# Graph attention on one core: PSUM copies moved from VectorE to ScalarE in the 8-head layers, and reciprocals split from their small products

## The chip, the cores and the metric

The kernel runs on one core of a Trainium2 chip. The time is device microseconds of one execution. Five engines work side by side: TensorE (PE in the profile; its weight loads are PEld), VectorE (DVE), ScalarE (ACT), GpSimd (POOL) and SyncE (SP, which only issues transfers here). Matrix products are written to PSUM, which has eight banks per partition; DVE and ACT copy them from there to SBUF, the working memory.

## The reference, cut to what matters

Four graph layers follow one another on 3327 nodes with 512 features. Each is wrapped as `x = layernorm(x + layer(x, adj))`. Layers 0 and 2 are graph attention with 8 heads of 64 features, layer 3 with 4 heads of 128; layer 1 averages over the first 64 neighbours. The change touches the attention layers:

```python
def _L2_gnn_ref(h, adj, W, a):                      # layer 0 is the same without elu
    Wh = (h @ W).reshape(n, H, D)                   # H = 8, D = 64
    s1 = jnp.einsum('nhd,hd->nh', Wh, a1)
    s2 = jnp.einsum('nhd,hd->nh', Wh, a2)
    e = jax.nn.leaky_relu(s1[:, None, :] + s2[None, :, :], negative_slope=0.2)
    att_logits = jnp.where(adj[:, :, None] > 0, e, NEG_BIG)
    attention = jax.nn.softmax(att_logits, axis=1)
    h_prime = jnp.einsum('ijh,jhd->ihd', attention, Wh)
    return jax.nn.elu(h_prime.reshape(n, H * D))
```

## The kernel before

**The attention without a softmax pass.** With f1 and f2 the two scores of a node, the weight exp(leaky_relu(f1_i + f2_j)) is exp(f1_i) * d_j * max(r_i, q_j), with r = exp(-0.8 f1), q = exp(0.8 f2) and d = exp(0.2 f2). The factor of i cancels in the quotient. So a tile `t` = max(r_i, q_j) * mask (DVE, one instruction, line 396) times v_j = d_j Wh_j gives the sums: products `po` on PE (line 405). The denominators need only to know which side of the maximum won: ACT turns `t` into a step `y` in 8 bits (line 399), and PE multiplies it by pieces of d and d*q (`pd`, line 365).

**Units.** Nodes are padded to 3328 = 26 tiles of 128. The receiving nodes i are cut into two halves of 1664 = 13 tiles, the features into 4 slots of 128: two heads per slot in the 8-head layers (`HS == 2`), one in the 4-head layer. One call of `unit` handles one half and one slot: 8 calls per attention layer, 24 in all. A unit has 26 steps j, one per tile of sending nodes. Per step and head there is one `t` of 128 x 1664 on DVE, one `y` on ACT, and four `po` products, one per PSUM bank (the 1664 columns are cut as 448, 448, 384, 384). At odd j from 3 on, the `pd` products of steps j-3 and j-2 follow; those of the last two steps come after the loop.

**Buffers.** `t` has 3 buffers per head (6 in the 8-head layers), `y` 7 in layer 0, 8 in layer 2 and 4 in layer 3. The row vectors r, spread over all partitions (`rb`, 832 KB each by DMA, issued by POOL), have HS + 1 = 3 buffers in the 8-head layers: the first head of the next unit is loaded ahead, the second when the present unit's first head has been used for the last time. The `po` banks have one buffer each, so the next unit's `po` products wait for the copies of this unit's.

**Between units.** After the loop the four `po` banks are copied to `ob`: bank 0 by DVE (line 423), banks 1 to 3 by ACT (line 421). After the last slot of a half the denominators are copied from the two `pd` banks to `db`: the lower 64 partitions by ACT (line 452), the upper 64 by DVE (line 453). What is left is returned as a list of jobs that run inside the *next* unit, one per step j, behind that step's `po` and `pd` products: two empty ones, then (after a half) `reciprocals`, then transposes of `ob` (`pt`, copied to `hb` and stored to `hd`) at every second step. `reciprocals` is 26 records of small products `pe` from `db` on PE (line 460), then on DVE, per head of a slot, a multiplication (line 468) and an addition (line 469), and one reciprocal (line 471) into `rec`. After the last unit of a layer the jobs run one after the other.

**Order.** The instruction order on PE is the order of the program text (`manual_schedule` for that engine). On DVE, ACT, POOL and SP a planner orders the instructions when the program is built, by dependencies and its own time estimates; `tc.keep_in_program_order(ins)` ties one instruction behind the instruction that was traced before it on the same engine. At the end of layers 0 and 2 the finishing work of the first two node tiles (`finish`: division by `rec`, layer norm, and elu in layer 2, lines 180 to 194 and 152 to 161) is traced in the last unit, and the planner places parts of it in earlier units.

Of the kernel before, what the change touches and what calls it, by code (L numbers as in the profile page):

```python
# [13 lines left out]
ALU = mybir.AluOpType  # L14
# [18 lines left out]
def kernel(  # L33
# [10 lines left out]
    nc = tc.nc  # L44
# [11 lines left out]
    WA, WB = NA * P, IW - NA * P  # L56
# [48 lines left out]
    for e in range(2):  # L105
        nc.vector.tensor_tensor(c1w[:, :, e, :], c1[:, :, 8 * e:8 * e + 4], c1[:, :, 8 * e + 4:8 * e + 8],
                                op=ALU.add)
# [115 lines left out]
    class Layer:  # L223
# [121 lines left out]
        def unit(self, pools, half, s, background, aside, final=None, ending=None):  # L345
            H, D, HS = self.H, self.D, self.HS
# [4 lines left out]
            for h in heads:  # L351
                r_ = rp.tile([P, IW], F32, name="rb")
# [6 lines left out]
            pd, seen = self.pd, self.seen  # L359
# [57 lines left out]

            ob = sp.tile([P, IW], F32, name="ob", bufs=1)
            for c, (a_, z) in enumerate(CUTS):
                if c:  # L420
                    nc.scalar.copy(ob[:, a_:z], po[c][:, :z - a_])
                else:
                    nc.vector.tensor_copy(ob[:, a_:z], po[c][:, :z - a_])
# [17 lines left out]
            nothing = lambda: None  # L441
            jobs = [nothing, nothing]
# [5 lines left out]
            db = sp.tile([P, WA], F32, name="db", bufs=1)  # L448
            if WB < WA:
                nc.gpsimd.memset(db[64:, WB:], 0.0)  # L450
            for c in range(2):
                nc.scalar.copy(db[:64, c * (WA // 2):(c + 1) * (WA // 2)], pd[c][:64, :WA // 2])
                nc.vector.tensor_copy(db[64:, c * (WB // 2):(c + 1) * (WB // 2)], pd[c][64:, :WB // 2])

            def reciprocals():
                pe = qp.tile([P, HALF, 2, H], F32, name="pe", tag="q")
                for q in range(HALF):
                    e = int(q >= NA)
                    cc = c1[:, :, 8 * e:8 * e + 8] if HS == 2 else c1w[:, :, e, :]
                    nc.tensor.matmul(pe[:, q, :, :], db[:, (q - e * NA) * P:(q - e * NA + 1) * P], cc,  # L460
                                     start=True, stop=True)

                ss = slice(0, NS) if not final else slice(0, 2) if s == 1 else slice(s, s + 1)
                r_ = rec[:, t0:t0 + HALF, :H].rearrange("p t (s k) -> p t k s", k=HS)
                rc = self.rc[:, t0:t0 + HALF, :].rearrange("p t (s k) -> p t k s", k=HS)
                pv = pe.rearrange("p t o (k s) -> p t o k s", k=HS)
                for k in range(HS):
                    nc.vector.tensor_tensor(r_[:, :, k, ss], pv[:, :, 0, k, ss], rc[:, :, k, ss], op=ALU.mult)
                    nc.vector.tensor_tensor(r_[:, :, k, ss], pv[:, :, 1, k, ss], r_[:, :, k, ss], op=ALU.add)
                hs = slice(ss.start * HS, ss.stop * HS)  # L470
                nc.vector.reciprocal(rec[:, t0:t0 + HALF, hs], rec[:, t0:t0 + HALF, hs])

            return jobs[:2] + [reciprocals] + jobs[2:]

# [412 lines left out]
    with tc.tile_pool(name="col0", bufs=1) as cp, tc.tile_pool(name="raw", bufs=2) as rawp:  # L889
        L0.more_columns(cp)  # L890
        L0.piece_columns(cp)
        with tc.tile_pool(name="p_w", bufs=1, reuse_waits="tile") as wp, \
# [37 lines left out]
            held = {}  # L930
# [100 lines left out]
```

## Time and profile before

| | us |
|---|---|
| median of 3 runs | 3499.28 (3495.52 to 3499.89) |
| profiled execution, its own time | 3489.1 |
| its span, first to last instruction | 3486.7 |
| units 0 to 7 (layer 0), first `t` to last `t` | 160.8 to 985.9 |
| units 8 to 15 (layer 2) | 1837.5 to 2628.0 |
| units 16 to 23 (layer 3) | 2761.1 to 3447.7 |
| unit 5, from its first `t` to the next unit's | 97.98 |
| unit 4 (first of layer 0's second half) | 103.12 |
| unit 12 (first of layer 2's second half) | 102.71 |

The mean granted TensorE clock of the profiled execution is 0.983. In the profile's lines, `L396 DVE ... t<-rb,qc,mask` reads: line 396 of the kernel, on VectorE, writing tile `t` from `rb`, `qc` and `mask`; then shapes, the count, and busy time. In a timeline the first number is the start in microseconds from the span's start and the second the duration of the merged run of instructions; brackets give the idle time before and what ended it. Costs below come from this one execution; the changed kernel is compared by medians.

### The profile page before, as it was taken

Reading aid. Unit: us, or ns where it says so; the run is one execution under the profiler, and the core shown is the slowest. Engines: PE = TensorE matmul, PEld = TensorE weight load, DVE = VectorE, ACT = ScalarE, POOL = GpSimd, SP = SyncE. Lnnn points to the kernel's source line nnn. Section 1 sums busy time; section 2 is a strip of 40 time slices with the busy share of each in tenths; the row PEclk is TensorE's granted clock in tenths of the full one; section 3 lists DMA queues with packets and bytes.
Section 4 is the critical chain, followed back from the end, with each engine's and each line's share of the span. In section 5 each row is a group of like instructions: output and inputs, shape, how many; then the busy total and the mean of one; then the engine's idle time right before and its main releaser. Section 6 shows DMA issues by size and latency. Waiting matters only on the chain.

```text
span 3486.7 us, 48120 instructions
## 1 busy us (share of the span) xinstructions
PE 3325.6 (95%) x18873; PEld 1701.2 (49%) x18926; DVE 2694.9 (77%) x2759; ACT 2396.6 (69%) x2336; POOL 181.2 (5%) x289
## 2 busy tenths in 40 slices
PE   6899999999989999999998999999998999999997
PEld 5644444444444455555553444444446754555553
DVE  5599999999967644434439999999998756668886
ACT  1388989899953343433428999899998655558885
POOL 1000000000000111111110000000001000000000
PEclk9999999999999999999999999999999999999998
DMA  9535211101133432222221111111116511112211
GB/s 352 179 104 161 67 44 41 54 27 51 37 105 125 131 90 73 70 61 75 73 66 35 48 47 48 47 46 46 29 39 197 183 33 44 40 46 91 81 38 47
DMA packets 208452, 276.65 MB, mean 79 GB/s; under 512 B 19321, under 2 KB 140355, under 8 KB 208228
## 3 DMA queue, kind: packets, MB, share of 16 engines
q1 hardware_dynamic: 173622, 157.37, 14.1%
q0 software_dynamic: 22736, 89.80, 8.3%
q10 hardware_dynamic: 11870, 26.42, 2.4%
q8 instruction: 149, 2.44, 0.3%
q14 instruction: 75, 0.61, 0.1%
HBM read 204.92 MB, written 68.60 MB: 78 GB/s over the span
## 4 chain that ended last, share of the span: by engine, by line
PE 62%; issue 24%; DVE 6%; DMA 5%; ACT 3%; POOL 1%; POOLq 0%; DVEq 0%; SPq 0%; ACTq 0%
PE po L405 34%; PE acc L728 9%; PE pw L264 5%; PE pd L365 5%; DVE t L396 3%; PE pz L617 2%; PE pi L620 2%; DMA raw<-in_adjT_dram 2%; ACT y L399 1%; DMA cy<-ctd 1%; PE pt L429 1%; PE pk L696 1%; PE pt L253 1%; DVE kt L700 1%; PE pe L460 1%
## 5 line engine op out<-in xcount | busy, mean ns | idle before, releaser
L396 DVE SCALAR_TENSOR_TENSOR t<-rb,qc,mask 128x1664 f32<-128x1664 f32 x1040 | 1960.1, 1947 | 200.8 <-PE po L405 158.6
L399 ACT ACTIVATE y<-t,bi,sc 128x1664 fp8e4<-128x1664 f32 x1040 | 1771.7, 1766 | 341.4 <-PE pd L365 317.4
L405 PE MATMUL po<-t,vj 128*64 128x448 f32 (+3 forms) x8320 | 1939.5, 522 | 26.0 <-DVE t L396 24.6
L405 PEld LDWEIGHTS po<-t,vj 128*64 128x64 f32 (+1 forms) x8320 | 857.8, 148 | 977.7 <-issue 681.1
L728 PE MATMUL acc<-zs,kt 128*128 128x512 bf16 x1314 | 396.6, 381 | 1.9 <-issue 0.4
L264 PE MATMUL pw<-wsb,xT 128*128 128x264 f32 (+1 forms) x1248 | 299.3, 395 | 21.7 <-DVE vt L270 19.5
L688 ACT CAST pk<-cy 128x256 f32<-128x256 bf16 x338 | 124.0, 374 | 272.7 <-DVE kt L700 224.8
L728 PEld LDWEIGHTS <-kt 128*128 128x128 fp8e4 x2028 | 198.8, 98 | 229.6 <-issue 34.5
L264 PEld LDWEIGHTS pw<-wsb,xT 128*128 128x128 f32 x1248 | 238.9, 196 | 65.6 <-issue 18.8
L365 PE MATMUL pd<-y,sden 128*32 128x448 fp8e4 (+1 forms) x4160 | 259.8, 342 | 10.5 <-ACT y L399 10.5
L700 DVE SCALAR_TENSOR_TENSOR kt<-pk,mask 128x256 fp8e4<-128x256 f32 x338 | 140.9, 421 | 159.5 <-PE pk L696 158.9
L728 PE MATMUL acc<-zl,kt 128*128 128x512 bf16 x661 | 252.1, 381 | 1.1 <-DMA zl<-zd 0.5
L365 PEld LDWEIGHTS <-sden 128*32 128x32 bf16 x4160 | 117.8, 96 | 162.4 <-issue 139.8
L270 DVE TENSOR_TENSOR vt<-pw,dc 128x256 f32<-128x256 f32 x156 | 59.1, 418 | 98.1 <-ACT dc L265 93.5
L696 PE MATMUL pk<-mask,upto 128*128 128x256 fp8e4 x338 | 92.5, 274 | 21.1 <-ACT pk L688 20.0
L353 POOL DMA_DIRECT2D rb<-r x40 | 21.5, 539 | 1646.8 <-DVE t L396 1610.1
L268 ACT COPY fc<-pw 128x8 f32<-128x8 f32 (+1 forms) x156 | 22.8, 163 | 112.1 <-PE pw L264 101.8
L617 PE MATMUL pz<-wn,xT 128*128 128x512 f32 x208 | 95.0, 600 | 1.2 <-ACT xT L611 1.2
L620 PE MATMUL pi<-wl,xT 128*128 128x512 f32 x208 | 93.5, 592 | 0.0
L590 POOL DMA_DIRECT2D cy<-ctd x91 | 67.8, 745 | 400.2 <-ACT pk L688 273.5
L708 DVE SCALAR_TENSOR_TENSOR y<-acc,cnt,bnb 128x512 f32<-128x512 f32 x26 | 19.5, 751 | 85.1 <-PE acc L728 85.1
L524 DVE TENSOR_SCALAR mask<-raw 128x832 fp8e4<-128x832 int32 (+2 forms) x86 | 50.2, 592 | 45.0 <-DMA raw<-in_adjT_dram 44.4
(165 smaller groups left out, 1732.2 us busy)
## 6 DMA issues: line engine op xcount, KB each, us to landing
vj<-v SPq DMA_DIRECT2D x312, 128.0 KB
rb<-r POOLq DMA_DIRECT2D x40, 832.0 KB, 4.7
cy<-ctd POOLq DMA_DIRECT2D x78, 256.0 KB, 3.9
v<-vt SPq DMA_DIRECT2D x75, 256.0 KB
h<-hd SPq DMA_DIRECT2D x65, 256.0 KB
raw<-in_adjT_dram ACTq DMA_DIRECT2D x38, 416.0 KB
raw<-in_adjT_dram SPq DMA_DIRECT2D x37, 416.0 KB
hd<-hb SPq DMA_DIRECT2D x60, 256.0 KB
```

The source lines that it names most:

```text
L264: nc.tensor.matmul(pw[e][:, :FW + H], xT[:, c, :], wsb[:, c, e, :], start=c == 0, stop=c == FC - 1)
L365: nc.tensor.matmul(pd[c][32 * kk:32 * kk + 32, :w_], lhsT, rhs, start=(kk, c) not in seen, skip_group_check=final is not None, stop=last a ...
L396: nc.vector.scalar_tensor_tensor(t, rb[k], self.qc[:, j, h:h + 1], mask[:, j, i0:i0 + IW], op0=ALU.max, op1=ALU.mult)
L399: nc.scalar.activation(y, t, AF.Sigmoid, bias=self.bi[:, j, h:h + 1], scale=self.sc[:, j, h:h + 1], saturate=False)
L405: nc.tensor.matmul(po[c][k * D:(k + 1) * D, :z - a_], vj[:, j % 2, k * D:(k + 1) * D], ts[k][:, a_:z], start=j == 0, stop=j == NT - 1)
L590: nc.gpsimd.dma_start(out=cy[:, :n, :], in_=ctd[t:t + n, b * GW:(b + 1) * GW] .rearrange("(o t) i -> o t i", o=1).to_broadcast([P, n, GW]))
L617: nc.tensor.matmul(pz, xT[:, c, :], wn[:, c, :], start=c == 0, stop=c == FC - 1)
L620: nc.tensor.matmul(pi, xT[:, c, :], wl[:, c, :], start=c == 0, stop=c == FC - 1)
L688: nc.scalar.copy(pks[k % 2], carry[b, t // 4 * 4][:, t % 4, :])
L696: nc.tensor.matmul(pk, upto, mask[:, t, i0:i0 + GW], start=False, stop=True, skip_group_check=True)
L700: nc.vector.scalar_tensor_tensor(kt, pk, NEIGHBOURS, mask[:, t, i0:i0 + GW], op0=ALU.is_le, op1=ALU.mult, saturate=False)
L728: nc.tensor.matmul(acc, kts[t][:, s * P:(s + 1) * P], zs[:, t, c, :] if c < 2 else zl[:, t, :], start=t == 0 and c == 0, stop=t == NT - 1 ...
```

## The change

In the 8-head layers all four `po` banks are copied to `ob` by ACT, and both halves of `pd` are copied to `db` by ACT. In all attention layers `reciprocals` is split in two jobs: `sums` (the products `pe`, at the step where `reciprocals` stood) and `reciprocals` (the DVE operations), two steps later, with one empty job between; so the transposes after a half also come two steps later. The multiplications of line 468 are tied behind what was traced before them on DVE.

```diff
             for c, (a_, z) in enumerate(CUTS):
-                if c:
+                if c or HS == 2:
                     nc.scalar.copy(ob[:, a_:z], po[c][:, :z - a_])
                 else:
                     nc.vector.tensor_copy(ob[:, a_:z], po[c][:, :z - a_])
...
             for c in range(2):
                 nc.scalar.copy(db[:64, c * (WA // 2):(c + 1) * (WA // 2)], pd[c][:64, :WA // 2])
-                nc.vector.tensor_copy(db[64:, c * (WB // 2):(c + 1) * (WB // 2)], pd[c][64:, :WB // 2])
-
-            def reciprocals():
+                (nc.scalar.copy if HS == 2 else nc.vector.tensor_copy)(
+                    db[64:, c * (WB // 2):(c + 1) * (WB // 2)], pd[c][64:, :WB // 2])
+            held = []
+
+            def sums():
                 pe = qp.tile([P, HALF, 2, H], F32, name="pe", tag="q")
+                held.append(pe)
                 for q in range(HALF):
...
+            def reciprocals():
+                pe = held[0]
+
                 ss = slice(0, NS) if not final else slice(0, 2) if s == 1 else slice(s, s + 1)
...
                 for k in range(HS):
-                    nc.vector.tensor_tensor(r_[:, :, k, ss], pv[:, :, 0, k, ss], rc[:, :, k, ss], op=ALU.mult)
+                    tc.keep_in_program_order(
+                        nc.vector.tensor_tensor(r_[:, :, k, ss], pv[:, :, 0, k, ss], rc[:, :, k, ss], op=ALU.mult))
                     nc.vector.tensor_tensor(r_[:, :, k, ss], pv[:, :, 1, k, ss], r_[:, :, k, ss], op=ALU.add)
...
-            return jobs[:2] + [reciprocals] + jobs[2:]
+            return jobs[:2] + [sums, nothing, reciprocals] + jobs[2:]
```

## The prediction

> **What bounds the kernel now.** I read the page's busy shares first, then the table by stretches (one 8-head unit per stretch), then the timeline of VectorE (DVE) and ScalarE (ACT) at the start of unit 4 (layer 0, second half, slot 0), then the views of the tiles `rb`, `db` and `ob`, and last the two epilogues of the 8-head layers. A unit is one call of `unit`; I number the 24 calls in order of time: 0 to 7 are layer 0, 8 to 15 layer 2, 16 to 23 layer 3.
>
> ```profile
> PE 3325.6 (95%) x18873; PEld 1701.2 (49%) x18926; DVE 2694.9 (77%) x2759; ACT 2396.6 (69%) x2336; POOL 181.2 (5%) x289
> ```
> ```profile
> core 0: us, PE busy (x) PEld busy (x) DVE busy (x) ACT busy (x) POOL busy (x), PEclk, DMA share, GB/s
> 588.75:691.87 103.12, 101.86 (x728) 44.49 (x727) 99.78 (x61) 91.07 (x62) 1.25 (x3) 0.97 0.15 48
> 691.87:789.85 97.98, 97.79 (x702) 43.28 (x701) 97.98 (x55) 90.43 (x60) 1.06 (x2) 1.00 0.14 44
> 2133.15:2230.95 97.80, 97.01 (x673) 44.42 (x670) 97.48 (x54) 91.19 (x61) 1.06 (x2) 1.00 0.14 44
> 2230.95:2333.66 102.71, 101.34 (x728) 46.81 (x727) 99.79 (x62) 91.64 (x62) 1.26 (x3) 1.00 0.15 47
> ```
> Over the whole span TensorE (PE) looks like the bound. By unit it is not: in unit 5 (691.87 to 789.85) DVE is busy for all 97.98 us. Units 4 and 12, the first after a half, are longer by 5.1 and 4.9 us, and there DVE idles 3.3 and 2.9 us.
>
> ```profile
> 590.62 0.61 DVE L423 COPY ob<-po 128x448 f32<-128x448 f32 x1
> 591.72 5.68 DVE L396 SCALAR_TENSOR_TENSOR t<-rb,qc,mask 128x1664 f32<-128x1664 f32 x3 [0.48 <-DMA rb<-r]
> 597.42 1.03 DVE L453 COPY db<-pd 64x384 f32<-64x384 f32 x2
> 598.49 7.54 DVE L396 SCALAR_TENSOR_TENSOR t<-rb,qc,mask 128x1664 f32<-128x1664 f32 x4
> 608.82 0.21 DVE L468 TENSOR_TENSOR rec<-pe,rc 128x52 f32<-128x52 f32 x1 [2.79 <-PE pe L460]
> ...
> 615.60 3.71 DVE L396 SCALAR_TENSOR_TENSOR t<-rb,qc,mask 128x1664 f32<-128x1664 f32 x2
> ```
> The columns are start, duration, instruction, and in brackets the idle time before it with what ended it. Three things to see: the copy L423 is followed by a wait for the DMA of `rb`; the two copies L453 stand between two `t`; L468 waits 2.79 us for the small products. ACT and PE beside it:
>
> ```profile
> 591.66 1.25 ACT L421 COPY ob<-po 128x448 f32<-128x448 f32 x3
> 593.18 3.44 ACT L399 ACTIVATE y<-t,bi,sc 128x1664 fp8e4<-128x1664 f32 x2 [0.27 <-PE pd L365]
> 596.53 0.94 ACT L452 COPY db<-pd 64x448 f32<-64x448 f32 x2
> 597.36 10.11 ACT L399 ACTIVATE y<-t,bi,sc 128x1664 fp8e4<-128x1664 f32 x6
> 615.88 1.77 ACT L399 ACTIVATE y<-t,bi,sc 128x1664 fp8e4<-128x1664 f32 x1 [8.41 <-PE pd L365]
> ```
> ```profile
> 595.48 6.55 PE L405 MATMUL po<-t,vj 128*64 128x448 f32 x34
> 602.36 3.01 PE L405 MATMUL po<-t,vj 128*64 128x448 f32 x14 [0.33 <-DVE t L396]
> 605.30 3.48 PE L460 MATMUL pe<-c,db 128*128 128x16 f32 x26
> ```
> So here PE waits for DVE (0.33 us) and ACT for PE; DVE sets the pace. One `t` costs DVE (5.68 - 1.95) / 2 = 1.865 us from start to start, and 52 of them 97.0 us of a unit's 98. Against that, the Trainium skill (Perfetto Trace Analysis, Identifying the Most-Contended Engine) says to work on the engine of highest occupancy, while warning that matmul busy time is no good measure for TensorE. By its first half the change, which takes nothing off PE, would give 0 us; the table by unit speaks for the warning.
>
> **Part 1, `ob` copy c = 0 from DVE to ACT, 16 units.** Off DVE go 16 x 0.61 = 9.9 us busy (0.53 each from start to start). Little of it is on the path. The view of `rb` over units 4 to 7 gives:
>
> ```profile
> DMA to landing us min/median/max: 4.2/4.4/5.2
> ```
> The second head's `rb` of the next unit is loaded into the buffer that t(25,0) frees: t(25,0) ends at 586.9, POOL issues at 587.25, the data lands at 591.62. DVE has two `t` to do meanwhile (t(25,1) and the next t(0,0)) and would be ready at 590.6. A hole of 1.0 us stays whatever stands in it: today 0.53 of copy and 0.48 of wait, afterwards 1.0 of wait. Gain 0 at the boundaries that show such a wait. At six (into units 5 to 7 and 13 to 15) the planner also put a 0.6 us step of the finishing work there, so copy plus step take 1.13: the gain is 0.1 each, 0.6 together. If these steps go elsewhere, 6 x 0.5 = 3 us are lost instead.
>
> On ACT a fourth `ob` copy adds 1.25 / 3 = 0.42 us between two `y`, ahead of the last `y` of the unit; the last `pd` products wait for that `y`, and the next unit's first `po` for them. PE thus starts 0.14 (the present 0.27 us of ACT idle absorbs the rest) to 0.42 us later. Cover: `t` has 6 buffers, three steps. In units 2, 3, 5 to 7 and 9 to 15 each `t` begins at least 3.1 us after `y` and `po` had freed its buffer (starts and ends from the timeline), so DVE does not feel it. Cost 0.
>
> **Part 2, `db` upper halves from DVE to ACT, 4 times.** In units 4 and 12 DVE loses L453 between two `t`: 598.49 - 597.36 = 1.13 us each, on the path. ACT gets 2 x 0.47 = 0.94, ahead of the first `y` of the unit; y(3,1) waits 8.4 us for PE anyway, which hides it.
>
> **Part 3, small products and reciprocals apart.** `sums` stays where `reciprocals` was on PE (step 2); DVE's part comes two steps later, behind t(4,1). Unit 4 forward: `rb` lands as before, t(0,1) starts at 591.72; nine `t` later (no L453) DVE is at 591.72 + 9 x 1.865 = 608.5. PE: `po` of steps 0 and 1 from 595.6 to 595.9 on, 6.0 us; t(2,1) ends at 601.1, so step 2 runs at once, to 604.5 to 605.0; `pe` 3.41 more: 607.9 to 608.4. The pinned L468 then waits for nothing, by 0.1 us at the tight end. The five DVE operations cost 1.2 us interleaved, as now, t(5,0) 1.865: t(5,1) starts at 611.6 where it starts at 615.60 now. **Gain 4.0** (2.79 + 1.13 + rounding). Unit 12 the same way: 2233.90 + 16.8 = 2250.7, t(5,1) at 2253.75 instead of 2257.38: **3.6** (2.38 + 1.13).
>
> What is late next: y(3,1) (layer 0 has 7 `y` buffers) waits for the first `pd` products of the unit, which follow step 3 on PE. With `pe` done at 608.3 and 3.0 for step 3, they begin at 611.3, y(3,1) at 612.7 (1.43 after, as now) and ends at 614.5; t(6,1), which takes over the buffer of t(3,1), would start at 611.6 + 3.7 = 615.3. Margin 0.8, today 1.6. If it is gone, DVE idles up to about 1 us there; between 0 and 1.0 I take 0.4, the value if PE starts at its late end. Layer 2 has 8 buffers and margin to spare. The transposes and the `hd` stores move two steps too (PE 0.6, ACT 0.57 and one SP issue every second step): these fall on PE and ACT beside DVE-bound steps, and nothing reads `hd` until later. The 4-head layer gets only the later, pinned reciprocals; there DVE waits on PE (17.1 us of idle before `t` in unit 23 alone), so 0.
>
> **Part 4, the two epilogues.** No `t` follows, so the copies are on the path to `pe`. Layer 0: ACT copies at 995.99 and 996.40, DVE's at 996.54 and 997.05, `pe` from 997.16. With all on ACT and one more `ob` copy ahead, the first pair ends at 995.99 + 0.42 + 0.94 = 997.35 instead of 997.10: +0.2 to +0.4. Layer 2: DVE's first copy is late (2635.54, behind finishing work), ACT could be through at 2635.3: up to -0.8. The view of `db` shows why ACT in series costs so little:
>
> ```profile
>   ACT db L452: 9.0, 4
> ```
> DVE's copy of a bank waits for ACT's of the same bank; they alternate already. The Trainium skill (PSUM — Partial Sum Buffer, Terms, "Quadrant") reports that different quadrants of one bank may be accessed at once. By that the halves could overlap and two more ACT copies would cost their full 0.94 us in each epilogue; no overlap shows here. Against both stands the planner's choice of where the square-root and exponential tables load: layer 0's epilogue has two loads of 1.28 us ahead of the last `y`. Bounds: -2.6 to +2.6, I take 0.
>
> **The sum.** -4.0 - 3.6 - 0.6 + 0.4 = -7.8 us. The profiled execution took 3489.1 (span 3486.7 and 2.4 around it), so 3481.3 there; the median of the runs is 10.2 above the profiled one, and the same step gives 3499.28 - 7.8 = **3491.5**. Bounds of this case: best -7.6 - 0.6 - 2.6 = -10.8 (3488.5); worst -7.6 + 1.0 + 3.0 + 2.6 = -1.0 (3498.3).
>
> **Rivals.** (a) *The wait comes back elsewhere* (PE late into `pe`, or the missing `y`): then only 2 x 1.13 and little more remain, 3496 to 3499. For it: margins of 0.1 and 0.8 us. Against: PE's own work in unit 4 is 26 x 2.85 for `po` (start to start of unhindered steps) + 15 for `pd` + 1.9 + 3.4 = 94.4 us, under DVE's 99. (b) *Slower: ACT becomes the bound where it changes tables.* Place: units 5 to 7 and 13 to 15 and the epilogues, where finishing work puts square root or exponential between the `y`. Price: two loads, 2.6 us, plus the new copy's 0.42. The margin is 3.1 us (3.4 in unit 13), so it decides where two such detours, or one plus a late last `y`, meet in one unit start. In all six, 6 x 2.6 = 15.6 - 7.8 = +7.8: 3507. Against: ACT is busy only 90 of 98 us. (c) *The `ob` copy counts in full*, 16 x 0.53 = 8.5 more: 3483. It needs `rb` to land 0.5 us earlier, and nothing moves its issue.
>
> **Chances.** Forecast case 0.60, (a) 0.20, (b) 0.16, (c) 0.04. 0.2% is 7.0 us, about what a measurement of this kernel can tell from no change; the forecast is just beyond. Of its 0.60 I put 0.46 beyond 7.0 and 0.14 within: faster 0.46 + 0.04 = 0.50, same 0.14 + 0.20 = 0.34, slower 0.16. The range goes from 3486 (2.5 below the case's best, toward (c)) to 3502 (half of the way from its worst into (b)), which leaves out (c) and most of (b).
>
> **What would show it.** Right: no wait before L468 in units 4 and 12, their first-`t` distances at 99.1 us, units 9 to 11 still 97.8 to 98.1 with the wait for `rb` near 1.0. Wrong: DVE idle on `y` or `po` in units 4 to 7, units without copy at 97.3 (then `rb` was not the limit), more table loads among the `y`, or an L468 that still waits.

## The result, and the profile after

The changed kernel takes 3493.66 us (median of 4 runs, 3489.95 to 3497.12) where the kernel before took 3497.40 in the same comparison: ratio 0.9992, 95% interval 0.9973 to 1.001. Two later comparisons with 11 runs each gave 0.9991 (0.9983 to 1.0000) and 0.9992 (0.9983 to 1.0001). So it is some 3 us faster, under 0.1%, and each of the three intervals still touches no change. The profiled execution of the changed kernel was the longest of its four: 3497.12 us, span 3495.1. Its page says nothing about where 3 us went:

```profile
PE 3324.9 (95%) x18873; PEld 1696.7 (49%) x18926; DVE 2683.9 (77%) x2735; ACT 2409.5 (69%) x2363; POOL 181.3 (5%) x289
```

DVE has 11.0 us less to do, ACT 12.9 more, and the span did not follow. The table by stretches, units 4, 5, 11 and 12 as before (the second number is the distance from first `t` to first `t`):

```profile
core 0: us, PE busy (x) PEld busy (x) DVE busy (x) ACT busy (x) POOL busy (x), PEclk, DMA share, GB/s
591.75:690.64 98.89, 97.90 (x728) 43.37 (x727) 98.03 (x58) 92.44 (x65) 1.25 (x3) 0.98 0.15 49
690.64:788.70 98.06, 97.82 (x702) 43.25 (x701) 98.06 (x55) 90.89 (x61) 1.06 (x2) 1.00 0.14 44
2131.74:2229.85 98.11, 97.01 (x673) 44.15 (x670) 96.94 (x54) 91.63 (x62) 1.06 (x2) 1.00 0.14 44
2229.85:2329.32 99.47, 98.76 (x728) 43.80 (x727) 98.04 (x59) 92.44 (x65) 1.26 (x3) 0.98 0.16 49
```

Units 4 and 12 are 4.2 and 3.2 us shorter, as forecast. Units 5 and 11 are not shorter at all, though each lost its copy: in unit 11 DVE idled 97.80 - 97.48 = 0.32 us before, and now 98.11 - 96.94 = 1.17. The timeline of VectorE at the start of unit 4 shows both (line 476 is the former 468, 477 the former 469):

```profile
586.16 7.53 DVE L396 SCALAR_TENSOR_TENSOR t<-rb,qc,mask 128x1664 f32<-128x1664 f32 x4
594.55 16.85 DVE L396 SCALAR_TENSOR_TENSOR t<-rb,qc,mask 128x1664 f32<-128x1664 f32 x9 [0.86 <-DMA rb<-r]
611.32 0.21 DVE L476 TENSOR_TENSOR rec<-pe,rc 128x52 f32<-128x52 f32 x1
611.44 1.94 DVE L396 SCALAR_TENSOR_TENSOR t<-rb,qc,mask 128x1664 f32<-128x1664 f32 x1
```

Nine `t` in a row, no copy between them, and an L476 that waits for nothing: Part 3. But ahead of them the hole is still there. Before, 0.61 us of copy and 0.48 of wait filled it; now 0.86 of wait alone. ScalarE and TensorE beside it:

```profile
594.65 1.68 ACT L421 COPY ob<-po 128x448 f32<-128x448 f32 x4
596.23 3.45 ACT L399 ACTIVATE y<-t,bi,sc 128x1664 fp8e4<-128x1664 f32 x2
599.57 0.52 ACT L452 COPY db<-pd 64x448 f32<-64x448 f32 x1
600.10 0.47 ACT L453 COPY db<-pd 64x384 f32<-64x384 f32 x1
...
601.64 10.10 ACT L399 ACTIVATE y<-t,bi,sc 128x1664 fp8e4<-128x1664 f32 x6
616.06 3.44 ACT L399 ACTIVATE y<-t,bi,sc 128x1664 fp8e4<-128x1664 f32 x2 [4.32 <-PE pd L365]
```
```profile
598.53 8.60 PE L405 MATMUL po<-t,vj 128*64 128x448 f32 x48
607.06 3.07 PE L463 MATMUL pe<-c,db 128*128 128x16 f32 x26
```

The four `ob` copies take 1.68 us on ACT, where three took 1.25, and ACT still waits 4.32 us for PE later in the unit. `pe` ends at 610.13, and L476 starts at 611.32: a margin of 1.2 us here.

What the unit table does not show is the rest of the span. The profile was taken twice of the kernel before and three times of the changed one; means in us, cut at the first and last `t` of each attention layer:

| stage | before | after | difference |
|---|---|---|---|
| start to the first `t` | 162.5 | 162.7 | +0.3 |
| layer 0, units 0 to 7 | 826.5 | 820.8 | -5.6 |
| of it unit 4 | 103.2 | 99.1 | -4.1 |
| epilogue of layer 0, layer 1, up to layer 2's first `t` | 850.4 | 851.1 | +0.7 |
| layer 2, units 8 to 15 | 792.0 | 789.5 | -2.5 |
| of it unit 12 | 102.8 | 99.4 | -3.3 |
| last `t` of layer 2 to first `t` of layer 3 | 135.0 | 141.4 | **+6.4** |
| layer 3, units 16 to 23 | 686.6 | 689.4 | **+2.7** |
| tail | 38.9 | 38.6 | -0.3 |

By these profiles layers 0 and 2 won 8.1 us, and the two stages in bold gave 9.1 back. (A single profiled execution scatters: the same program showed 161.8 to 164.6 us up to the first `t`, and all rows together come out 1.7 us slower, where the timed runs say 3 faster. The sizes that follow are therefore taken from runs with timing where there are any.)

### The profile page after: what moved, and what is told of

Read it like the earlier page. It is cut to its first block, busy times and chain, and to the rows that moved or that the text cites. A ratio compares the mean times of both kernels' runs of the same rounds, so it can differ in the third digit from the quotient of the medians.

```text
span 3495.1 us, 48134 instructions
## 1 busy us (share of the span) xinstructions
PE 3324.9 (95%) x18873; PEld 1696.7 (49%) x18926; DVE 2683.9 (77%) x2735; ACT 2409.5 (69%) x2363; POOL 181.3 (5%) x289
## 3 DMA queue, kind: packets, MB, share of 16 engines
q8 instruction: 149, 2.44, 0.3%
## 4 chain that ended last, share of the span: by engine, by line
PE 65%; issue 19%; DVE 7%; DMA 5%; ACT 3%; POOL 1%; POOLq 0%; SPq 0%; DVEq 0%; ACTq 0%
PE po L405 38%; PE acc L736 9%; PE pd L365 5%; PE pw L264 4%; DVE t L396 4%; PE pz L625 2%; PE pi L628 2%; DMA raw<-in_adjT_dram 2%; ACT y L399 1%; DMA cy<-ctd 1%; PE pt L429 1%; PE pk L704 1%; DVE kt L708 1%; PE pe L463 1%; PE pt L253 1%
## 5 line engine op out<-in xcount | busy, mean ns | idle before, releaser
L696 ACT CAST pk<-cy 128x256 f32<-128x256 bf16 x338 | 124.0, 374 | 270.4 <-DVE kt L708 220.7
```

The costliest lines, as they stand in the source:

```text
L696: nc.scalar.copy(pks[k % 2], carry[b, t // 4 * 4][:, t % 4, :])
```

## The experiments

The theory: the units behave as predicted; the removed copy leaves a hole that the transfer of `rb` sets; and the gain of units 4 and 12 is given back in the stage ahead of layer 3, by the planner's order there, and in layer 3, by the split. The rivals: the copy's gain went to ACT or PE; and the missing microseconds are scatter.

**The changed kernel again**, for the scatter.

> The changed kernel once more, unaltered. Theory A (the new order that the planner gave the finishing work costs time): the stretch between layer 2's last t and layer 3's first t, 133.1 us before and 142.6 in the first profile of the changed kernel, is 141 to 144 again, layer 3 again about 689, units 4 and 12 again 98.9 and 99.5. Theory B (these were scatter between executions, like the 3.9 us by which the first t came later though nothing ahead of it was changed): the stretch comes back at 133 to 138. Total: A 3491 to 3496, B 3487 to 3491.

Measured: 3495.00 us against 3497.48, ratio 0.9991 (0.9983 to 1.0000). Units 4 and 12 at 99.2 and 99.4, the stage ahead of layer 3 at 141.7, layer 3 at 690.0. The two slower stages repeat. The first `t`, 3.8 us later in the first profile of after than in the first of before, is at 161.8 here: that was scatter.

**The split alone**: all copies on the engines that had them before.

```diff
-                if c or HS == 2:
+                if c:
...
-                (nc.scalar.copy if HS == 2 else nc.vector.tensor_copy)(
+                nc.vector.tensor_copy(
```

> Only the split of the small products and the reciprocals, with the pin; all copies as before. Theory A: the wait of L468 goes and nothing else: unit 4 from 103.1 to 100.2 (minus 2.8 to 2.9), unit 12 from 102.7 to 100.2 (minus 2.4 to 2.5), other 8-head units unchanged at 97.8 to 98.2. Rival (the wait comes back at y or po): units 4 and 12 at 102 or more. The total depends on the order of the finishing work, which may differ again.

Measured: 3491.23 us, 0.9987 (0.9979 to 0.9996). Units 4 and 12 at 100.6 and 100.8: the split alone brings 2.6 and 2.0 of their 4.1 and 3.3 (100.2 was expected; the wait for `rb` is 0.72 and 0.92 us in these two units, 0.48 in each in the first profile of the kernel before). The stage ahead of layer 3 is 134.6, layer 3 689.2. So the layer-3 loss belongs to the split, and the loss ahead of layer 3 does not. Half of the change is as fast as all of it, within the intervals.

**The copies alone**: `reciprocals` in one piece, as before.

```diff
-            return jobs[:2] + [sums, nothing, reciprocals] + jobs[2:]
+            return jobs[:2] + [reciprocals] + jobs[2:]
```

> Only the copies to ScalarE; reciprocals undivided and unpinned as before. Theory A: PE's small products end 0.4 to 0.9 us earlier at most (their start depends on t(2,1), 1.1 us earlier, and on po of steps 0 and 1, 0.1 to 0.4 us later), so L468 waits longer, about 3.2, and units 4 and 12 gain 0.4 to 0.9 each: 102.2 to 102.7 and 101.8 to 102.3. Rival (the two copies count in full without the split): 101.5 and 101.1. Interior units unchanged, 97.8 to 98.2, in both; with a longer wait in place of the ob copy.

Measured: 3496.16 us, 0.9996 (0.9987 to 1.0004). The timeline of VectorE in its unit 4:

```profile
592.94 13.13 DVE L396 SCALAR_TENSOR_TENSOR t<-rb,qc,mask 128x1664 f32<-128x1664 f32 x7 [1.34 <-DMA rb<-r]
608.45 0.21 DVE L468 TENSOR_TENSOR rec<-pe,rc 128x52 f32<-128x52 f32 x1 [2.38 <-PE pe L460]
```

The wait for `pe` stays (2.38 us, where about 3.2 was expected), the hole is 1.34 us of waiting, and units 4 and 12 are at 101.9: between the two expectations in unit 4, as expected in unit 12. Layer 3 is as before (686.6), the stage ahead of it is 138.5.

**Is it really `rb` that holds the first `t`?** The second head's `rb` goes into the buffer that t(25,0) frees. In the last two steps the first head's two `t` are made first, so that buffer comes free one `t` (1.87 us) earlier; nothing else is changed from the kernel after:

```diff
+                if HS == 2 and j == NT - 2:
+                    for k, h in enumerate(heads):
+                        weigh(j, k, h)
+                        weigh(j + 1, k, h)
+                elif HS == 1 or j < NT - 2:
+                    for k, h in enumerate(heads):
+                        weigh(j, k, h)
```

(`weigh` holds the two instructions of lines 396 and 399.)

> The changed kernel, and in the 8-head layers t(24,1) and t(25,0) change places, so that the buffer for the second rb of the next unit comes free one t (1.87 us) earlier. Theory A (the hole at the start of a unit is the rb transfer): the wait of 0.9 to 1.4 us in front of t(0,1) goes, and units from first t to first t fall from 98.1 to 96.9 to 97.2 where no finishing step stands in between, about 10 to 12 us in both 8-head layers together. Rival (the hole is PE's or ScalarE's lateness, as the labels po and y on some of these waits say): no gain, 98 again. A cost that could show: po of step 24 waits 1.87 us longer, PE ends the unit up to 0.8 us later, inside its margin of over 3 us.

Measured: 3479.93 us, 0.9949 (0.9938 to 0.9961), the largest effect of the study until then. The timeline of VectorE across the end of unit 5:

```profile
773.99 13.12 DVE L396 SCALAR_TENSOR_TENSOR t<-rb,qc,mask 128x1664 f32<-128x1664 f32 x7
```

One run of `t` across the boundary, without hole, and units 3, 6, 7, 10, 14 and 15 take 96.9 us, which is 52 x 1.863. This shows that the prediction's hole was the transfer's. Units 5, 9, 11 and 13 kept a wait (97.9 to 98.6): there the transfer itself took 6.2 to 6.8 us, against 4.4 to 5.0 in the six units named (last section). So layers 0 and 2 together are 7.5 us shorter in this profile than in the changed kernel's, not the 10 to 12 expected; the profiled execution was the longest of its six. The planner also puts no finishing step into the starts of units 5 to 7 and 13 to 15 any more, so a part of what these units lose is work that is done elsewhere.

**And the copy, once the hole is gone?** The same, with the `ob` copy c = 0 back on DVE (`if c:`).

> The kernel with the early rb, with one thing put back: ob bank 0 is copied by VectorE again in the 8-head layers. Theory A (the ob copy cost nothing only because the rb wait covered it): at the boundaries where e4 showed no hole (units of 96.9) the copy now stands on the path, 97.4 to 97.5 (plus 0.53); where e4 still waited 1.0 to 1.7 us for rb, units stay at e4's 97.9 to 98.6. Rival (the copy is free in any case): 96.9 again. Against the changed kernel both 8-head layers together still gain 2 to 7 us.

Measured: 3489.16 us, 0.9986 (0.9977 to 0.9995). The timeline of VectorE at the same boundary:

```profile
783.80 5.67 DVE L396 SCALAR_TENSOR_TENSOR t<-rb,qc,mask 128x1664 f32<-128x1664 f32 x3
789.60 0.62 DVE L431 COPY ob<-po 128x448 f32<-128x448 f32 x1
790.14 1.94 DVE L396 SCALAR_TENSOR_TENSOR t<-rb,qc,mask 128x1664 f32<-128x1664 f32 x1
```

Now the copy stands between two `t`, 0.67 us from the end of the one to the start of the other (790.14 - 789.47), and units without a wait are at 97.60 instead of 96.85: it costs 0.75 us, not the 0.53 expected. So Part 1 of the change is worth nothing behind a late `rb` and about 0.75 us a boundary behind an early one. The two kernels differ by 0.0037, some 13 us, more than the 16 x 0.75 = 12 of all boundaries, and at some the wait remains; their profiles differ by 7.4 us in layers 0 and 2. Where the rest goes was not found. In these two layers the kernel is as long as the changed kernel in the mean (1610.3 against 1610.4 us); 2 to 7 us of gain were expected.

**The order ahead of layer 3.** On ACT and DVE this stage has one order in the kernel before and in the split-only kernel, and another in the kernel after and the copies-only kernel. With the copies on ACT only in the units of the first half, the earlier order comes back, while units 4 and 12 keep everything:

```diff
-                if c or HS == 2:
+                if c or HS == 2 and half == 0:
...
-                (nc.scalar.copy if HS == 2 else nc.vector.tensor_copy)(
+                (nc.scalar.copy if HS == 2 and half == 0 else nc.vector.tensor_copy)(
```

> The changed kernel, but the copies move to ScalarE only at the ends of the first half's units; the second half's ob and db copies stay as before, so that units 5 to 7, 13 to 15 and both epilogues give the planner the same holes as before. Theory A (the copies of the second half made the planner pull other finishing steps forward, and the projection stage of layer 3 then ran in a worse order): that stage returns from 142 to 133 to 135, while units 4 and 12 keep 98.9 to 99.5; layer 3 stays at 689 to 690; total 8 to 9 us under the changed kernel, 3485 to 3488. Rival (anything that moves layer 2's end by some us gives another order): the stage lies anywhere from 136 to 143.

Measured: 3489.00 us, 0.9982 (0.9971 to 0.9993); stage 135.9, a little above the 133 to 135 expected, units 4 and 12 at 99.1 and 99.4. By the ratios that is some 3 us under the changed kernel, not 8 to 9. Since this interval still touched the changed kernel's, both ran again side by side, 11 runs each, with the kernel before profiled a second time.

> The kernel before, profiled a second time. Order theory (the stage between layer 2's last t and layer 3's first t is shorter because of the order of ACT's and DVE's instructions in it, which this kernel shares with the split-only and the first-half-copies kernels: 133.1, 134.6, 135.9 us so far): this stage 132 to 137 us. Rival, scatter between executions (the other order showed 137.2 to 142.6): anywhere from 133 to 143. Layer 0 823 to 826 us, layer 2 788 to 792, units 4 and 12 at 102.5 to 103.5, both with a wait ahead of L468.

> The changed kernel once more, on the same chip as the next one. Order theory: stage ahead of layer 3 137 to 143 us; time 2 to 4 us under the kernel before, ratio 0.999. Rival, scatter: the same time as the next kernel within 1.5 us.

> The changed kernel with the copies on ACT only at the end of the units of the first half (units 0 to 3 and 8 to 11); in the others they stay where they were before. Units 4 and 12 keep their gain, and the order of ACT and DVE in the stage ahead of layer 3 is that of the kernel before. Order theory: this stage 132 to 137 us, the time 4 to 7 us under the changed kernel's of this call, ratio to before 0.9975. Rival, scatter: within 1.5 us of the changed kernel.

Measured: kernel before, stage 137.0, at the upper end of what was expected (layers 0 and 2, at 827.7 and 793.6, lie 1.7 and 1.6 us above it); changed kernel 3493.47 us, stage 140.0; first-half copies 3489.25 us, 0.9974 (0.9965 to 0.9983), stage 136.2. The difference of these two kernels' means is 5.1 us (95% 2.6 to 7.6), which holds whatever the second half's copies cost or save as well. Over the study the earlier order showed 133.1, 137.0, 134.6, 135.9 and 136.2 us, the later one 142.6, 141.7, 140.0, 138.5 and 137.2: means 135.4 and 140.0, with only 0.2 us between the nearest two. The granted TensorE clock of the stage explains much of the scatter inside each order:

| kernel | stage, us | PE busy | PE idle | clock |
|---|---|---|---|---|
| before, first profile | 133.1 | 119.9 | 13.2 | 0.95 |
| before, second profile | 137.0 | 123.3 | 13.7 | 0.91 |
| split alone | 134.6 | 121.3 | 13.3 | 0.94 |
| first-half copies, first profile | 135.9 | 119.3 | 16.6 | 0.95 |
| first-half copies, second profile | 136.2 | 120.8 | 15.4 | 0.94 |
| after, first profile | 142.6 | 125.1 | 17.4 | 0.92 |
| after, second profile | 141.7 | 124.0 | 17.7 | 0.93 |
| after, third profile | 140.0 | 121.9 | 18.1 | 0.94 |
| copies alone | 138.5 | 120.5 | 18.0 | 0.95 |
| split in the 8-head layers only (below) | 137.2 | 119.8 | 17.4 | 0.96 |

PE's idle time is 14.4 us in the mean of the earlier order and 17.7 in the later one, with 16.6 and 17.4 the nearest two. These 3.3 us go with the order; the other 1.3 of the 4.6 are PE busy longer, and the longest busy times stand beside the lowest clocks. Where PE idles can be read in the changed kernel's third profile. By stretches, then TensorE, then ScalarE:

```profile
core 0: us, PE busy (x) PEld busy (x) DVE busy (x) ACT busy (x) POOL busy (x), PEclk, DMA share, GB/s
2700.00:2730.00 30.00, 23.96 (x125) 19.33 (x123) 27.19 (x77) 23.00 (x52) 4.28 (x8) 1.00 0.62 209
```
```profile
2727.86 0.66 PE L253 MATMUL pt<-ident,h 128*128 128x128 f32 x4 [1.08 <-ACT h L161]
2730.40 5.43 PE L264 MATMUL pw<-wsb,xT 128*128 128x260 f32 x16 [1.89 <-ACT xT L255]
```
```profile
2720.63 1.28 ACT L154 ACT_TABLE_LOAD   x1
2723.03 0.30 ACT L154 ACTIVATE rs<-mv,eps 128x2 f32<-128x2 f32 x1 [1.11 <-DVE mv L153]
2725.18 1.28 ACT L185 ACT_TABLE_LOAD   x1 [1.85 <-DVE rs L155]
...
2728.56 0.60 ACT L255 COPY xT<-pt 128x512 f32<-128x512 f32 x1
```

ACT loads the square root's table, waits 1.11 us for DVE's variances `mv`, and stands idle for another 1.85 us ahead of the exponential's load. The label names DVE's reciprocal `rs`, but the exponential (L185) reads `h`, which DVE delivers 0.08 us before the load starts:

```profile
2724.42 0.68 DVE L180 TENSOR_TENSOR h<-h,rec 128x512 f32<-128x512 f32 x1
```

The copy of the transposed tile `xT` stands behind all that, and PE stops twice, for 1.08 and 1.89 us. The same place in the kernel with first-half copies:

```profile
2700.00:2726.00 26.00, 24.10 (x127) 20.20 (x126) 24.51 (x74) 20.37 (x46) 3.05 (x6) 1.00 0.72 225
```
```profile
2726.00 0.60 PE L253 MATMUL pt<-ident,h 128*128 128x128 f32 x4
2726.54 3.75 PE L264 MATMUL pw<-wsb,xT 128*128 128x260 f32 x16
```
```profile
2726.63 0.58 ACT L255 COPY xT<-pt 128x512 f32<-128x512 f32 x1
2727.24 1.28 ACT L154 ACT_TABLE_LOAD   x1
2728.53 0.29 ACT L154 ACTIVATE rs<-mv,eps 128x2 f32<-128x2 f32 x1
2729.90 1.28 ACT L185 ACT_TABLE_LOAD   x1 [1.08 <-issue]
```

PE does as much (24.10 against 23.96 us busy) in 26 us as the other order in 30. Here ACT's square root finds its input ready, and ACT idles 1.08 us in this step instead of 2.96. The number of table loads doesn't explain the difference: the slower order has 27 of them in the stage, the faster 28. On their price the Trainium skill (ScalarE: Activation LUTs, What ACT_TABLE_LOAD costs) gives 1.28 us for the load and 1.38 us for a drain. The rows show the 1.28 and no drain: the load at 2727.24 starts 0.03 us after the copy ahead of it ends, and the activation 0.01 us after the load ends.

**The split in the 8-head layers only**: for `HS == 1` the job list is `jobs[:2] + [lambda: (sums(), reciprocals())] + jobs[2:]`, without the tie.

> The changed kernel, but the split and the pin only in the 8-head layers; the 4-head layer has its reciprocals in one job as before. Theory A (the two later steps cost the 4-head layer 2.4 to 3.4 us, in units 20 and 22, less a gain in unit 21): layer 3 returns to 686 to 687 with units 20, 21, 22 at 90.9, 84.9, 85.5. Rival (layer 3 suffers from what came before it, other offsets of the transfers or other order at its start): 689 to 690. The projection stage stays at about 142. Total 2 to 3 us under the changed kernel.

Measured: layer 3 at 685.0 us, units 20 to 22 back at 90.9, 84.9 and 85.5 as before; the stage ahead of it at 137.2, not 142. The time, however, 3494.91 us, 0.9997 (0.9987 to 1.0008), is not shorter than the changed kernel's 0.9991 and 0.9992. The interval of some 3.7 us either way is wider than the 2.7 us in question. So the loss in layer 3 is shown in its stage, in all eight profiles with the split there (687.6 to 690.0 us, mean 689.1) and in none of the six without (685.0 to 686.7, mean 686.4), and not in the whole.

Units 20 to 22, before and after (changed kernel, third profile):

```profile
3101.80:3192.71 90.91, 90.91 (x439) 48.13 (x435) 69.02 (x66) 69.94 (x55) 2.90 (x6) 0.98 0.26 82
3192.71:3277.60 84.89, 84.89 (x359) 42.95 (x352) 69.00 (x68) 74.53 (x61) 4.11 (x8) 1.00 0.27 84
3277.60:3363.12 85.52, 84.61 (x348) 43.95 (x348) 71.67 (x78) 80.21 (x65) 5.24 (x9) 1.00 0.20 65
```
```profile
3105.14:3197.76 92.62, 92.62 (x450) 48.95 (x443) 66.94 (x63) 66.91 (x52) 2.90 (x6) 0.98 0.26 79
3197.76:3280.09 82.33, 82.33 (x339) 41.47 (x337) 69.40 (x69) 78.53 (x64) 3.77 (x7) 1.00 0.28 87
3280.09:3369.01 88.92, 87.14 (x353) 45.09 (x351) 73.69 (x81) 81.88 (x67) 5.60 (x9) 0.98 0.20 63
```

Unit 20 is 1.7 us longer and unit 21 2.6 shorter, as PE work moves from the one to the other (450 and 339 matmuls, formerly 439 and 359). In unit 22 both DVE and PE do more, and 3.4 us are lost: PE is busy 2.5 us longer and idles 1.8 us where it idled 0.9. Which operation sets that was not tried.

**Early `rb`, first-half copies and the 8-head split together.**

> Early rb, the split and the pin in the 8-head layers only, the copies to ScalarE in the first half only. If the parts add: layer 0 about 817, layer 2 about 788 (the second half pays 0.5 us per ob copy again where rb comes in time), layer 3 686 to 687, projection stage 133 to 142 (with the hole at the start of a unit gone, the planner may place the finishing steps in yet another way, as it did in e4). Total 3472 to 3482, faster than every version so far if the stage comes out under 140.

Measured: 3484.47 us, 0.9972 (0.9963 to 0.9981), over the 3472 to 3482 expected and not the fastest: no sum of gains. Layer 3 is 686.6, but the stage ahead of it is 144.7, in yet another order of its instructions, and with an early `rb` the second half's copies on DVE stand on the path again, as the kernel with the copy back on DVE had shown.

**Early `rb` and the 8-head split, all copies on ACT.**

> The changed kernel with the first head's t of the last step ahead of the second head's t of the step before (so that the transfer of rb starts one t earlier), and with the split of reciprocals in the 8-head layers alone. If the split costs 2.4 us in layer 3 and an earlier rb gives 1.2 us at each boundary where the wait goes: layer 3 686.6 us, layers 0 and 2 as in the kernel with the early rb alone (816 and 787), 3477.5 us, ratio 0.9942. Rival (the cost in layer 3 is made good later): 3480, ratio 0.995.

Measured: **3476.35 us, 0.9941 (0.9928 to 0.9953)**, 20.6 us under the kernel before and 17 under the changed one, the fastest of the study; layer 3 686.6, layer 2 780.9, the stage ahead of layer 3 136.1. Whether keeping the split to the 8-head layers adds anything to the early `rb` (0.9949 with the split everywhere) cannot be told from these intervals. Its units 4, 5, 11 and 12:

```profile
589.60:689.22 99.62, 97.88 (x729) 44.05 (x727) 98.31 (x59) 92.54 (x65) 1.25 (x3) 0.98 0.16 49
689.22:786.07 96.85, 95.86 (x703) 41.34 (x701) 96.85 (x53) 90.85 (x61) 1.06 (x2) 1.00 0.15 46
2125.04:2221.91 96.87, 96.05 (x672) 43.69 (x669) 96.87 (x54) 91.42 (x62) 1.06 (x2) 1.00 0.14 45
2221.91:2319.99 98.08, 97.26 (x729) 42.74 (x727) 98.04 (x58) 92.52 (x65) 1.25 (x3) 0.98 0.16 50
```

DVE is busy in all of units 5 and 11: nothing is left there but the `t` themselves. In unit 4 the early `rb` uses up the margins of Part 3: DVE now waits 0.59 us for `pe`, 0.39 for PE's `po` and 0.33 for ACT's `y`. One reading limits the order theory: this kernel has in the stage ahead of layer 3 the same order as the kernel with the early `rb` alone, and they showed 136.1 and 141.1 us (PE busy 122.4 and 125.3, idle 13.7 and 15.8, clock 0.92 and 0.90). A single profile can be 5 us off, and 2 us by PE's idle time.

## Why the prediction was right, and where not

The time predicted, 3491.5, is 2.2 us under the measured 3493.66, and the range holds it. But the forecast case put 7.8 us off, and 3 to 4 were found; by the 0.2% bound the outcome is the one without a difference, which had 0.34, and not "faster" with 0.50. There is luck in the 2.2 us: the prediction started from a median of 3499.28 of the kernel before, which came out as 3497.40 in the comparison, so 1.9 of the 4.1 us of missing gain don't show. And the range of 3486 to 3502 would have held no change at all. What speaks for the prediction is its mechanism in the units, not its total.

**Part 1, the hole behind the copy: right in the mechanism.** Nothing was won at the boundaries, the wait for `rb` took the copy's place, and the early `rb` showed both sides of it. The size has the other sign: at the six boundaries with finishing steps, instead of -0.1 each, units 5 to 7 and 13 to 15 went from a mean of 98.07 (two profiles) to 98.29 (three), since two steps of 1.3 us together now stand where copy and one step took 1.13. Units 9 to 11 went from 97.92 to 98.15; there the second head's transfer took 4.52 us instead of 4.32 in the mean, for which no reason was found. (16 x 0.61 is 9.8, not 9.9; nothing rests on it.)

**Parts 2 and 3: right.** -4.1 and -3.3 us measured against -4.0 and -3.6. No wait before L476 in either unit; the allowance of 0.4 for the late y(3,1) was not needed (ACT waits 4.32 us there, and DVE waits for no `y`). Alone, the split brings about 60% of it and the copies 1.3 and 0.9, since without the split DVE still waits 2.38 us for `pe` in unit 4. The total of 3 us lies nearer to rival (a)'s "2 x 1.13 and little more" than to the forecast's 7.8, but not by rival (a)'s mechanism: no wait came back in these units.

**Part 4, the epilogues: the step that failed.** "Bounds: -2.6 to +2.6, I take 0" was priced by the loads of tables on ACT. What the copies cost directly was small: the small products `pe` begin 11.56 us after the last `t` of layer 0 instead of 11.24, as forecast, and 8.49 instead of 8.16 in layer 2, where up to 0.8 us less was thought possible; so the upper halves' copies did not cost their full 0.94 us. But the planner made a new order of the stage ahead of layer 3, in which ACT waits for DVE between two loads and PE for ACT. The stage is 4.6 us longer in the mean of five profiles each, 3.3 of it as idle time of PE: beyond the bound. (The 5.1 us of the side-by-side runs agree, but hold the second half's other differences too.) What was not seen: where the copy stood, the planner puts more of the finishing work. Before, units 13 to 15 held the copy and one full step each (L180, L191, L192); after, they hold two (twice L180, then L192 and L191, then L152 and L191, 1.3 us each), and with the copy back in those units it is one again. So an edit in the units reorders a stage that it hardly touches. That the extra steps in the units are what led the planner to the new order is argued from these placements; the runs show only that order and placement change together. The clause "If these steps go elsewhere" looked at the units only.

**The 4-head layer: also a failed step.** "So 0" rested on 17.1 us of DVE idle time. That was read in unit 23, and the loss is in units 20 and 22: the stage is 2.7 us longer in the mean of the profiles with the split. There PE and DVE wait for each other in turn, and idle time of DVE is no proof that its work is off the path. On the whole time this is not separated from scatter.

The sum with both: -7.8 + 4.6 + 2.7 = -0.5, inside the measured interval of -6 to 0. Rival (b), ACT as the bound in units 5 to 7 and 13 to 15, did not occur: these units are 0.2 us longer, not 2.6. Rival (c) is wrong for this kernel and right for one with an early `rb`.

The tie of line 476 has no part in any of this: without it the built program has the same instruction order on every engine.

On the Trainium skill's rule of the most contended engine (Perfetto Trace Analysis, Identifying the Most-Contended Engine): its first half, to work on the engine of highest occupancy, would have left these units alone, with PE at 95%. Its warning about matmul busy time was the better guide. The change itself hardly tells the two apart, with 3 us, but the fastest kernel takes 20.6 us off while PE stays at 95%:

```profile
PE 3311.8 (95%) x18873; PEld 1678.2 (48%) x18926; DVE 2682.2 (77%) x2735; ACT 2400.2 (69%) x2356; POOL 181.2 (5%) x289
```

## What to carry to other kernels

Work taken from the bounding engine is worth only what no wait takes up in its place: look for the transfer that lands last at the same point, and move its issue first; here this turned 3 us into 18 to 21. Where a planner orders the instructions, compare its order in every stage before and after, also in those that the edit does not touch, because freed time draws other work in. And try the parts of a change one by one: here one half alone was as fast as the whole, within the intervals.

## What was not expected of the hardware

The transfer of `rb` (832 KB) is not steady. In the kernels before and after it lands 4.2 to 5.4 us after its issue between 489 and 885 us. In the profile of the kernel with the early `rb`, the second head's transfer at five ends of units (0, 4, 8, 10 and 12) took 6.2 to 6.8 us:

```profile
DMA to landing us min/median/max: 6.2/6.4/6.7
```

This is the view of `rb` for the end of unit 4 (680 to 692 us), where two were issued, the second for a unit further on. At four of those five ends a packet of the queue that the profile lists as `q8 instruction` (149 packets, 2.44 MB, so 16 KB each) started within about 1 us of the issue, at the fifth only 5.9 us after it. At the ends of units 2, 6 and 14 such a packet started within 1.2 us and left the transfer at 4.85 to 5.04 us. The six transfers of this profile (ahead of units 2, 4, 6, 10, 12 and 14) during which none started took 4.4 to 4.6 us. In the kernel with all three parts together one transfer took 5.5 us without such a packet. So it is an association; what stretches the transfer stays open.
